# One more pair of row tiles per batch by half-size products in an attention and feed-forward block, with the turns and statistics moved to suit

## The chip, the cores and the metric

The kernel runs on one core of one Trainium2 chip. The metric is the device time of one execution in microseconds (us), of which the median over runs is given; lower is better. All arithmetic is 32-bit float. The core's engines each work through a list of instructions in order and wait for one another by semaphores: TensorE (PE in the profile, with PEld for its weight loads), VectorE (DVE), ScalarE (ACT), GpSimd (POOL) and SyncE (SP), which here only issues DMAs.

## What is computed

For each of 8 batches `b`, `x[b]` is 1024 x 256. The reference, cut to what matters:

```python
mod = (_silu(c) @ wmod).reshape(8, 6, 1, -1)
sa, ca, ga, sb, cb, gb = (mod[:, n] for n in range(6))     # ga, gb are kept away from zero
h = _layernorm(x) * (1 + ca) + sa
scores = einsum('nsd,ntd->nst', h * w_lhs, h * w_rhs)      # per batch 1024 x 1024
x = x + ga * einsum('nst,ntd->nsd', softmax(scores), h)
h = _layernorm(x) * (1 + cb) + sb
x = x + gb * (relu(h @ W1 + b1) @ W2 + b2)                 # 256 -> 1024 -> 256
```

## The kernel before, in words

**Tiles and order.** A batch has eight row tiles `i` of 128 rows, in two halves `g` of four (TH = 4). The loop at the end of the kernel goes over `b`, then over `i`, and in step (b, i) it writes out, in the order in which they are to run, the scores of tile i + 2 (`direct`, with `mirror`, since the scores are symmetric), the maximum (`row_max`), its turn onto columns by PE (`max_turn`), `subtract` and `exponent` of tile i + 1, the attention product of tile i, and a part of the feed-forward network (FFN) of the batch before: steps 0, 1 do its first product for half 0 (four chunks `c`, two in each step), steps 2, 3 its second product, steps 4 to 7 the same for half 1. The last batch's FFN runs after the loop. `pin` at the end ties each engine's instructions to the order in which they were written, so no scheduler changes it: what is behind a waiting instruction on its engine waits too. In batch 0 the attention is done differently and is not touched.

**The attention product.** `product(b, i)` (lines 486 to 499) multiplies the weights `pT` of one tile, as eight blocks of 128 x 128, with eight tiles of `xg`, 257 columns wide (256 and a column of ones for the softmax's denominator), into `po`. `product_out` (501 to 510) divides on DVE, adds to `x` and takes the statistics of the row (`stats`, lines 236 to 240) for the second layernorm, into `mvb`.

**Pairs.** Two tiles can be done together by a scheme of Strassen's kind with seven half-size products. `paired` (519) says which: i % 4 >= 2, so tiles 2 and 3, and 6 and 7, in batches 1 to 7. `pair_begin` (534) does two of the products (`pp`) on the first tile's weights alone, `pair_begin_sum` (553) adds them on DVE into `W`; `left_sums` (558) makes on POOL, in place, four sums of the two tiles' weights, of 128 x 512 each; `pair_end` (570) does the other five products (`pq`, `pr`), whose other side `tsum` comes from `right_sums` (once per batch); `pair_out` (589) puts them together on DVE in eight instructions; `pair_stats` (616) takes the statistics of both.

**FFN.** `pair_products` (722) does for one chunk the six products pa, pa, pb, pb, pc, pc and calls `between`, which holds the next `max_turn`, between pb and pc; ACT copies `pa` to `kept` (737); `pair_sums` (745) makes four DVE sums, `pair_last` (763) one more product, a DVE sum (769) and a POOL sum (770); `pair_relu` is ACT (779, 780), `pair_turn` (784) four POOL sums. The second product is `y_first`, `y_first_sums`, `y_second`, `y_second_sums` (843: two ACT instructions on Y). `y_turn` (848) transposes Y on DVE in blocks of 32 into a tile `T_y`, and `move` (296) sends it over DRAM: four DMAs out, one back, all issued by SP. With `hurry` the read back is issued at once, otherwise with the next move that hurries. `y_add` (860) adds it to `x` on POOL, `y_out` (868) stores.

**Turn buffers.** The tiles T of all transposes (`T_a`, `T_f`, `T_y`, `Tm`; lines 318, 429, 851) share one tag with two buffers, so a transpose waits until the DMAs out of the tile before the last have landed. PSUM tiles `pa`, `pb`, `pc`, `pp`, `pq`, `pr`, `po`, `ya` to `yd` share the four banks of the pool `ps_a`.

**The next batch's preparation** lies in the same steps: statistics at i = 1 and 3 (`prepare_stats`), the norm on ACT at i = 2 and 3 (`prepare_norm`, line 279), the turn and move (`prepare_blocks`) at i = 2 for half 0 and i = 4 for half 1, and the scaling on ACT (`prepare_turn_apart`, 340) at i = 4 and 5. `later` puts POOL work in a queue from which `spare` takes one piece.

Of the kernel before, what the change touches and what calls it, by code (L numbers as in the profile page):

```python
# [24 lines left out]
def adaln_block_kernel(  # L25
# [288 lines left out]
    def turn_blocks(src, name, X=None):  # L314

        T = two.tile([P, NV, NT * V], F32, tag="T", name=f"T_{name}")
        for k in range(ND):
            nc.vector.transpose(  # L320
                T.rearrange("p b (k t v) -> p k b t v", k=ND, v=V)[:, k],
                src(k).rearrange("p t (b v) -> p b t v", v=V),
            )
        if X is None:
            X = two.tile([P, NV, NT * V], F32, tag="X", name=f"X_{name}", bufs=1)
        move(X, T, NT * V, name)
        return X.rearrange("p a (k t v) -> p k t a v", k=ND, v=V)
# [94 lines left out]
    def mirror(b, i):  # L422
        if i == NT - 1:
            return
        n = NT - 1 - i
        if b == 0:
            mirror_first(i)
            return
        T = two.tile([P, NV, NT * V], F32, tag="T", name=f"Tm_{b}_{i}")
        T = T.rearrange("p b m -> p (b m)")[:, : NV * n * V].rearrange(  # L430
            "p (b m) -> p b m", b=NV
        )
        nc.vector.transpose(  # L433
            T.rearrange("p b (j v) -> p b j v", v=V),
            sc_t[b][:, i + 1 :, :, i, :].rearrange("p j b v -> p b j v"),
        )
        move(
            sc_t[b][:, i, :, i + 1 :, :].rearrange("p a j v -> p a (j v)"), T, n * V,
            f"m{b}_{i}",
        )  # L440
# [41 lines left out]

    mvb_t, po_t = {}, {}

    def product(b, i, parts=(0, 1)):
        pT = pT_t[b, i]
        if 0 in parts:
            po_t[b, i] = ps_a.tile([P, HALF], F32, tag="a", name=f"po_{b}_{i}")
        po = po_t[b, i]
        if 1 in parts:  # L490
            pT_t.pop((b, i))
        for t in [t for p in parts for t in range(p * TH, (p + 1) * TH)]:
            nc.tensor.matmul(  # L493
                po[:, : D + 1],
                lhsT=pT[:, t, :],
                rhs=xg_t[b][:, t, 0 : D + 1],
                start=(t == 0),
                stop=(t == NT - 1),
            )

    def product_out(b, i):
        po = po_t.pop((b, i))
        g, j = divmod(i, TH)
        if j == 0:
            mvb_t[b, g] = work.tile([P, TH, 2], F32, tag="mvb", name=f"mvb_{b}_{g}")
        rl = work.tile([P, 1], F32, tag="rl", name=f"rl_{b}_{i}")
        nc.vector.reciprocal(rl, po[:, D : D + 1])
        x2 = x_tile(b, i)
        nc.vector.scalar_tensor_tensor(x2, po[:, :D], rl, x2, ALU.mult, ALU.add)  # L509
        stats(mvb_t[b, g], j, x2, f"b{b}_{i}")  # L510

# [2 lines left out]
    XS = D - P + 1  # L516
    tsum = const.tile([P, 4, TH, P + 4], F32, name="tsum")
    nc.gpsimd.memset(tsum[:, 1, :, P : P + 1], 1.0)
    paired = lambda b, i: b > 0 and i % TH >= 2

    def right_sums(b, which):

# [47 lines left out]
    def pair_end(b, i):  # L570

        (s2, s4), (s3, a22) = halves(pT_t.pop((b, i))), halves(pT_t.pop((b, i + 1)))
        s1 = two_t.pop("s1")
        pq = ps_a.tile([P, HALF], F32, tag="a", name=f"pq_{b}_{i}")
        pr = ps_a.tile([P, HALF], F32, tag="a", name=f"pr_{b}_{i}")
        for out, lhs, rhs in (
            (pr[:, P : 2 * P], s1, tsum[:, 0, :, 0:P]),
            (pr[:, 2 * P : 3 * P], s3, tsum[:, 2, :, 0:P]),
            (pq[:, 0:XS], s2, tsum[:, 1, :, 0:XS]),
            (pq[:, XS : XS + P], a22, tsum[:, 3, :, 0:P]),  # L580
            (pr[:, 0:P], s4, xg_t[b][:, TH:NT, 0:P]),
        ):
            for t in range(TH):
                nc.tensor.matmul(  # L584
                    out, lhsT=lhs[:, t, :], rhs=rhs[:, t, :],
                    start=(t == 0), stop=(t == TH - 1),
                )
        two_t[b, i] = two_t[b, i][0], pq, pr
# [26 lines left out]

    def pair_stats(b, i):
        two_t.pop((b, i))
        g, j = divmod(i, TH)
        for q in range(2):
            stats(mvb_t[b, g], j + q, x_tile(b, i + q), f"b{b}_{i + q}")  # L620


    ffn = {}
# [96 lines left out]
    def pair_products(b, g, c, between=None):  # L720
# [12 lines left out]
        pc = ps_a.tile([P, HALF], F32, tag="a", name=f"pc_{b}_{g}_{c}")  # L733
        mm(pa[:, lo], w1[:, 0, n], hT[:, 0, lo])
        mm(pa[:, hi], s1, hs[:, 0])
        kept = work.tile([P, HALF], F32, tag="kept", name=f"kept_{b}_{g}_{c}", bufs=3)
        nc.scalar.copy(kept, pa)  # L737
        mm(pb[:, lo], w1s[:, 0, n], hs[:, 1])
        mm(pb[:, hi], w1s[:, 1, n], hs[:, 2])
        if between:  # L740
            between()
        mm(pc[:, lo], w1[:, 1, n], hT[:, 1, lo])
        mm(pc[:, hi], a22, hT[:, 0, hi])
        pairs[c] = pa, pb, pc, kept

    def pair_sums(b, g, c):
# [101 lines left out]
    def y_turn(b, g, hurry=False):  # L848

        Y = ffn["Y"]  # L850
        T = two.tile([P, NV, NT * V], F32, tag="T", name=f"T_y{b}_{g}")
        for h in range(2):
            nc.vector.transpose(
                T.rearrange("p a (t h u) -> p a t h u", h=2, u=V)[:, :, :, h, :],
                Y[:, h].rearrange("p (t a v) -> p a t v", a=NV, v=V),
            )
        Y = Y.rearrange("p h r -> p (h r)").rearrange("p (b m) -> p b m", b=NV)
        move(Y, T, NT * V, f"y{b}_{g}", hurry)
        ffn["rows", b, g] = Y.rearrange("p b (t h u) -> p t h b u", h=2, u=V)
# [239 lines left out]
    def middle(b, i):  # L1099

        if i == 0:
            ffn_norm(b - 1, 1)
        elif i == (6 if b < B - 1 else 4):
            ffn_norm(b, 0)

    def norms(b, i):
# [9 lines left out]
        elif b + 1 < B:  # L1116
# [3 lines left out]
            elif i == 2:  # L1120
                prepare_blocks(b + 1, 0)
                x_plus(b + 1, 0)
                xg_times(b + 1, 0)
        elif i == 4:

            ffn_blocks(b, 0)
        if b == B - 1:
# [12 lines left out]
    for b in range(B):  # L1140
        for i in range(NT):
# [59 lines left out]
            if first:  # L1201
# [3 lines left out]
                pair_products(fb, fg, c, turn_max)  # L1205
                if i == 0:
                    ffn_rstd(b - 1, 1)
                elif (b, i) == (B - 1, TH):
                    ffn_rstd(b, 0)
                if (b, i) == (1, 0):  # L1210
                    weights(*late)
                    late = None
# [3 lines left out]
                if ahead:  # L1216
                    mirror(*ahead)
                pair_last(fb, fg, c)
                if i == 0 and back:
                    for q in range(2):  # L1220
                        y_add(ub, ug, q)
                if i == TH + 1:
                    pair_turn(c - 1)
                if i == 4 and b + 1 < B:
                    prepare_blocks(b + 1, 1)
                    xg_times(b + 1, 1)
                if late:
                    subtract(*late)
                pair_products(fb, fg, c + 1, (lambda: max_turn(*extra)) if extra else None)
                if i == 5 and b + 1 < B:  # L1230
                    prepare_turn_apart(b + 1, 1, 1)
                    prepare_turn_apart(b + 1, 1, 0)
                pair_relu(c)
                sides_too = i == 4 and b + 1 < B
                if sides_too:
                    prepare_turn_apart(b + 1, 0, 1)
                if late:
                    exponent(*late)
                if sides_too:
                    prepare_turn_apart(b + 1, 0, 0)  # L1240
                middle(b, i)
                pair_sums(fb, fg, c + 1)
                pair_last(fb, fg, c + 1)
                if ahead and ahead != extra:
                    row_max(*ahead)
                pair_turn(c)
# [10 lines left out]
            else:  # L1257
                half = i % TH - 2
                if i == 3 and b + 1 < B:
                    prepare_stats(b + 1, 1)  # L1260
                if half == 0:
                    if i == 2:
                        pair_begin(b, i, turn_max)
                    else:
                        pair_begin(b, i, lambda: (max_turn(*late), weights(*late)))
                elif not ahead:

                    pair_end(b, i - 1)
                    pair_out(b, i - 1)
                    pair_stats(b, i - 1)  # L1270
                if half:
                    y_second(fb, fg, turn_max)
                else:
                    y_first(fb, fg)
                if i == NT - 2 and (b, 2) in two_t:
                    pair_stats(b, 2)
                if ahead:
                    mirror(*ahead)
                if i == 2 and b + 1 < B:
# [4 lines left out]
                    ffn_rstd(b, 0)  # L1284
                elif i == NT - 1 and b == B - 1:
                    ffn_rstd(b, 1)
                if half == 0:
                    pair_begin_sum(b, i)
                    if i == 2:
                        weights(*late)  # L1290
                    left_sums(b, i)
                spare()
                early(b, i)
# [22 lines left out]
            if not first:  # L1316
                if i == NT - 1 and b < B - 1:
                    y_turn(fb, fg, True)
                for _ in range(4 if half else 1):
                    spare()  # L1320
            if first:
                product(b, i)
                product_out(b, i)
            elif half and ahead:
                pair_end(b, i - 1)
                pair_out(b, i - 1)
                if i < NT - 1:
                    y_turn(fb, fg)
                if i == NT - 1:
                    assert not queue  # L1330
                    right_sums(b + 1, range(3))
                if i == NT - 1 or b == B - 1:
                    pair_stats(b, i - 1)
            late = ahead if ahead != extra else None
            if first and back:
# [82 lines left out]
```

## Time and profile before

| what | value |
|---|---|
| median of 3 runs | 772.51 us (772.37 to 774.09) |
| profiled execution, its own time | 774.46 us |
| its span in the trace | 772.7 us |
| PE busy | 759.6 us (98%) |
| DVE, POOL, ACT busy | 565.1, 538.2, 375.4 us |
| granted TensorE clock | 1.0 throughout |

One 32-bit product of the program is two PE instructions in the profile, so `product` shows as 16. Durations of one instruction overlap with the next; where times are added up, the distance from one start to the next is used. Times in the trace are us from the start of the span.

### The profile page before, as it was taken

To read this page: it belongs to the slowest core of one execution; us is meant where nothing else is said; L and a number is where in the kernel's file an instruction comes from. 1 tells how busy PE (TensorE), PEld (TensorE's weight loads), DVE (VectorE), ACT (ScalarE), POOL (GpSimd) and SP (SyncE) were. 2 spreads that over 40 slices of the span, in tenths; PEclk is the share of its full clock that TensorE was granted. 3 is DMA by queue.
4 is the path that set the end of the run, shared out by engine and by line. 5 is a ranking of instruction groups with operands and counts; after the bars stand their busy time and mean duration, and the time that the engine had idled before them with its cause. 6 is when DMAs were issued, how large, how long until landed. Compare 5 with 4: busy or idle time off the path is not lost.

```text
span 772.7 us, 11479 instructions
## 1 busy us (share of the span) xinstructions
PE 759.6 (98%) x3708; PEld 621.8 (80%) x3708; DVE 565.1 (73%) x1222; ACT 375.4 (49%) x681; POOL 538.2 (70%) x632
## 2 busy tenths in 40 slices
PE   8999999999999999999999999999999999999998
PEld 3576788788887888778887888878888788889886
DVE  6697878768785887758787687876878677595632
ACT  3464546635456355645546444563546535251511
POOL 4543974978849686596867787497884969559641
PEclk9999999999999999999999999999999999999999
DMA  5314335356443554434543554436534254142220
GB/s 193 123 50 145 106 103 133 101 176 170 123 122 101 171 143 113 140 95 151 156 126 118 150 150 130 117 101 192 167 93 130 87 167 142 35 115 98 81 83 27
DMA packets 106211, 95.18 MB, mean 123 GB/s; under 512 B 29700, under 2 KB 98848, under 8 KB 106152
## 3 DMA queue, kind: packets, MB, share of 16 engines
q1 hardware_dynamic: 98408, 85.81, 38.0%
q10 hardware_dynamic: 7744, 8.65, 3.7%
q8 instruction: 29, 0.48, 0.3%
q14 instruction: 30, 0.25, 0.1%
HBM read 50.62 MB, written 43.81 MB: 122 GB/s over the span
## 4 chain that ended last, share of the span: by engine, by line
PE 78%; DVE 10%; POOL 4%; DMA 3%; issue 2%; SPq 1%; ACT 1%; DVEq 0%; POOLq 0%
PE psc L410 14%; PE po L493 12%; PE pa L718 7%; PE yc L796 6%; PE ya L796 6%; PE yb L796 6%; PE pc L718 5%; PE pr L584 5%; PE pb L718 4%; PE pq L584 3%; PE py L901 3%; PE yd L796 3%; PE pp L544 3%; DMA D_y<-T_y 2%; DVE pT L472 1%
## 5 line engine op out<-in xcount | busy, mean ns | idle before, releaser
L770 POOL TENSOR_TENSOR f<-f,kept 128x512 f32<-128x512 f32 x64 | 81.5, 1273 | 116.7 <-DVE f L769 84.6
L410 PE MATMUL psc<-rT,lT 128*128 128x512 f32 (+3 forms) x384 | 134.6, 487 | 0.0
L493 PE MATMUL po<-xg,pT 128*128 128x257 f32 x576 | 131.6, 380 | 0.0
L493 PEld LDWEIGHTS po<-xg,pT 128*128 128x128 f32 x576 | 108.9, 190 | 15.9 <-issue 1.0
L472 DVE TENSOR_TENSOR pT<-sc,pm 128x1024 f32<-128x1024 f32 x64 | 77.1, 1205 | 30.7 <-PE pm L465 24.8
L410 PEld LDWEIGHTS psc<-rT,lT 128*128 128x128 f32 x384 | 67.7, 191 | 37.9 <-issue 26.3
L417 ACT COPY sc<-psc 128x512 f32<-128x512 f32 (+3 forms) x96 | 44.9, 475 | 104.0 <-PE psc L410 94.5
L481 ACT ACTIVATE pT<-pT 128x1024 f32<-128x1024 f32 x64 | 67.3, 1052 | 33.8 <-DVE pT L472 33.8
L460 DVE TENSOR_REDUCE m<-sc 128x1 f32<-128x1024 f32 x64 | 77.3, 1207 | 0.0
L737 ACT COPY kept<-pa 128x512 f32<-128x512 f32 x64 | 37.4, 584 | 78.2 <-PE pa L718 78.2
L779 ACT ACTIVATE f<-f 128x512 f32<-128x512 f32 x64 | 40.1, 627 | 62.4 <-POOL f L770 62.4
L718 PE MATMUL pb<-hs,w1s 128*128 128x256 f32 x256 | 66.0, 380 | 0.9 <-DVE f L755 0.8
L718 PE MATMUL pc<-hT,w 128*128 128x256 f32 x256 | 65.8, 380 | 0.0
L634 POOL TENSOR_TENSOR x<-x,rows 128x256 f32<-128x256 f32 x64 | 45.3, 739 | 22.3 <-DVE x L509 11.8
L718 PEld LDWEIGHTS pb<-hs,w1s 128*128 128x128 f32 x256 | 47.8, 190 | 9.1 <-DVE f L755 2.0
L718 PEld LDWEIGHTS pc<-hT,w 128*128 128x128 f32 x256 | 46.7, 192 | 6.9
L796 PE MATMUL yc<-f,w2s 128*128 128x256 f32 x224 | 52.1, 379 | 0.0
L796 PEld LDWEIGHTS yc<-f,w2s 128*128 128x128 f32 x224 | 41.5, 190 | 10.1 <-issue 2.9
L433 DVE STREAM_TRANSPOSE Tm<-sc 128x896 f32<-128x896 f32 (+6 forms) x49 | 34.6, 707 | 13.3 <-ACT sc L417 12.4
L790 POOL TENSOR_TENSOR ft<-ft,f 128x256 f32<-128x256 f32 x56 | 40.8, 728 | 4.4
L791 POOL TENSOR_TENSOR ft<-ft,f 128x256 f32<-128x256 f32 x56 | 40.8, 728 | 4.4
L789 POOL TENSOR_TENSOR ft<-f 128x256 f32<-128x256 f32 x56 | 40.9, 731 | 0.0
(165 smaller groups left out, 1672.7 us busy)
## 6 DMA issues: line engine op xcount, KB each, us to landing
D_f<-T_f SPq DMA_DIRECT2D x60, 128.0 KB, 2.7
X_f<-D_f SPq DMA_DIRECT2D x15, 512.0 KB, 3.7
D_a<-T_a SPq DMA_DIRECT2D x56, 128.0 KB, 3.2
D_y<-T_y SPq DMA_DIRECT2D x56, 128.0 KB, 2.6
Y<-D_y SPq DMA_DIRECT2D x14, 512.0 KB, 3.5
out_dram<-x SPq DMA_DIRECT2D x14, 512.0 KB, 3.0
X_a<-D_a SPq DMA_DIRECT2D x13, 512.0 KB, 3.4
x<-in_L_attn_x_dram ACTq DMA_DIRECT2D x12, 512.0 KB, 4.6
```

Of the source, the lines that this page charges most:

```text
L410: nc.tensor.matmul(psc[:, : hi - lo], lhsT=lT_t[b, i // TH][:, k, ts(i % TH, P)], rhs=rT_t[b, n][:, k, lo - n * HALF : HALF], start=(k == ...
L417: nc.scalar.copy(score_row(b, i)[:, lo // V : hi // V, :], psc[:, : hi - lo].rearrange("p (n v) -> p n v", v=V),)
L460: nc.vector.tensor_reduce(m, score_row(b, i), AX.XY, ALU.max)
L472: nc.vector.tensor_tensor(pT.rearrange("p j (a v) -> p j a v", v=V), score_columns(b, i), pm[:, :P].rearrange("p (j a v) -> p j a v", j=1, ...
L481: nc.scalar.activation(pT_t[b, i], pT_t[b, i], AF.Exp)
L493: nc.tensor.matmul(po[:, : D + 1], lhsT=pT[:, t, :], rhs=xg_t[b][:, t, 0 : D + 1], start=(t == 0), stop=(t == NT - 1),)
L584: nc.tensor.matmul(out, lhsT=lhs[:, t, :], rhs=rhs[:, t, :], start=(t == 0), stop=(t == TH - 1),)
L634: queue.append(lambda: nc.gpsimd.tensor_tensor(out, in0, row, op))
L718: nc.tensor.matmul(out, lhsT=lhsT, rhs=rhs, start=True, stop=True)
L770: nc.gpsimd.tensor_tensor(f[:, c::NH, hi], f[:, c::NH, hi], kept[:, None, hi].to_broadcast([P, 2, H2]), ALU.add,)
L789: add(ft[:, 0, c], f[:, c + NH, hi], f[:, c, hi], ALU.subtract)
L796: nc.tensor.matmul(out, lhsT=lhs(c), rhs=rhs(c), start=(c == 0), stop=(c == NH - 1))
```

## The change

Tiles 1 and 2, 3 and 4, 6 and 7 of batches 1 to 7 are done as pairs; tiles 0 and 5 by `product`. The middle pair spans both halves, so its statistics go to two tiles of `mvb`. `left_sums(b, 1)` stands at the start of step 2, `pair_end(b, 1)` at the end of step 2, `pair_begin(b, 3)` at the start of step 3, `pair_end(b, 3)` at the end of step 4. `y_turn` of half 0 goes from the end of step 3 into step 4, after the first chunk's `pair_last`; `prepare_blocks(b + 1, 1)` and `weights` (subtract and exponent) of tile 5 go behind the second chunk's `pair_last` of step 4; the exponent of tile 6 goes to before the scaling in step 5. T gets three buffers, `kept` two in place of three (one chunk of the last batch takes the buffer of `s1`), `between` is called after pc, the order of two products in `pair_end` changes, and in the last batch the norm of half 0 goes from step 4 to step 5.

```diff
-        T = two.tile([P, NV, NT * V], F32, tag="T", name=f"T_{name}")
+        T = two.tile([P, NV, NT * V], F32, tag="T", name=f"T_{name}", bufs=3)
...
+    def mvb_of(b, g):
+        if (b, g) not in mvb_t:
+            mvb_t[b, g] = work.tile([P, TH, 2], F32, tag="mvb", name=f"mvb_{b}_{g}")
+        return mvb_t[b, g]
...
-    paired = lambda b, i: b > 0 and i % TH >= 2
...
             (pr[:, P : 2 * P], s1, tsum[:, 0, :, 0:P]),
+            (pq[:, XS : XS + P], a22, tsum[:, 3, :, 0:P]),
             (pr[:, 2 * P : 3 * P], s3, tsum[:, 2, :, 0:P]),
             (pq[:, 0:XS], s2, tsum[:, 1, :, 0:XS]),
-            (pq[:, XS : XS + P], a22, tsum[:, 3, :, 0:P]),
...
-        g, j = divmod(i, TH)
-        for q in range(2):
-            stats(mvb_t[b, g], j + q, x_tile(b, i + q), f"b{b}_{i + q}")
+        for t in (i, i + 1):
+            stats(mvb_of(b, t // TH), t % TH, x_tile(b, t), f"b{b}_{t}")
...
-        kept = work.tile([P, HALF], F32, tag="kept", name=f"kept_{b}_{g}_{c}", bufs=3)
+
+        tag, bufs = ("s1", 1) if b == B - 1 and c % 3 == 2 else ("kept", 2)
+        kept = work.tile([P, HALF], F32, tag=tag, name=f"kept_{b}_{g}_{c}", bufs=bufs)
...
+        mm(pc[:, lo], w1[:, 1, n], hT[:, 1, lo])
+        mm(pc[:, hi], a22, hT[:, 0, hi])
         if between:
             between()
-        mm(pc[:, lo], w1[:, 1, n], hT[:, 1, lo])
-        mm(pc[:, hi], a22, hT[:, 0, hi])
...
-        elif i == (6 if b < B - 1 else 4):
+        elif i == (6 if b < B - 1 else 5):
             ffn_norm(b, 0)
...
-        elif i == 4:
+        elif i == 5:
             ffn_blocks(b, 0)
...
                 pair_last(fb, fg, c)
+                if (b, i) == (B - 1, 5):
+                    ffn_rstd(b, 0)
+                if i == 4:
+                    y_turn(fb, 0)
...
-                if i == 4 and b + 1 < B:
-                    prepare_blocks(b + 1, 1)
-                    xg_times(b + 1, 1)
-                if late:
+                if late and i != 4:
                     subtract(*late)
                 pair_products(fb, fg, c + 1, (lambda: max_turn(*extra)) if extra else None)
-                if i == 5 and b + 1 < B:
-                    prepare_turn_apart(b + 1, 1, 1)
-                    prepare_turn_apart(b + 1, 1, 0)
+                if i == 5:
+                    exponent(*late)
+                    if b + 1 < B:
+                        prepare_turn_apart(b + 1, 1, 1)
+                        prepare_turn_apart(b + 1, 1, 0)
...
-                if late:
+                if late and i not in (4, 5):
                     exponent(*late)
...
                 pair_last(fb, fg, c + 1)
+                if i == 4:
+                    if b + 1 < B:
+                        prepare_blocks(b + 1, 1)
+                        xg_times(b + 1, 1)
+                    weights(*late)
...
-                if half == 0:
-                    if i == 2:
-                        pair_begin(b, i, turn_max)
-                    else:
-                        pair_begin(b, i, lambda: (max_turn(*late), weights(*late)))
+                if i == 2:
+                    left_sums(b, 1)
+                elif i == 3:
+                    pair_begin(b, i, turn_max)
+                elif i == 6:
+                    pair_begin(b, i, lambda: (max_turn(*late), weights(*late)))
...
-                    y_second(fb, fg, turn_max)
+                    y_second(fb, fg, turn_max if i == NT - 1 else None)
                 else:
-                    y_first(fb, fg)
-                if i == NT - 2 and (b, 2) in two_t:
-                    pair_stats(b, 2)
+                    y_first(fb, fg, turn_max if i == 2 else None)
+                if i == NT - 2 and (b, 3) in two_t:
+                    pair_stats(b, 3)
...
-                if half == 0:
+                if i in (3, 6):
                     pair_begin_sum(b, i)
-                    if i == 2:
-                        weights(*late)
+                if i == 2:
+                    weights(*late)
+                elif i == 6:
                     left_sums(b, i)
...
-            if first:
+            if i in (0, 5):
                 product(b, i)
                 product_out(b, i)
-            elif half and ahead:
+            elif i == 1:
+                pair_begin(b, i)
+                pair_begin_sum(b, i)
+            elif i == 3:
+                left_sums(b, i)
+            elif i in (2, 4) or i == NT - 1 and ahead:
                 pair_end(b, i - 1)
                 pair_out(b, i - 1)
-                if i < NT - 1:
-                    y_turn(fb, fg)
                 if i == NT - 1:
                     assert not queue
                     right_sums(b + 1, range(3))
-                if i == NT - 1 or b == B - 1:
+                if i != 4 or b == B - 1:
                     pair_stats(b, i - 1)
```

More of the change, by code (lines that the diff above doesn't have):

```diff
@@ L428, in mirror @@
             return
-        T = two.tile([P, NV, NT * V], F32, tag="T", name=f"Tm_{b}_{i}")
+        T = two.tile([P, NV, NT * V], F32, tag="T", name=f"Tm_{b}_{i}", bufs=3)
         T = T.rearrange("p b m -> p (b m)")[:, : NV * n * V].rearrange(
@@ L503, in product_out @@
         g, j = divmod(i, TH)
-        if j == 0:
-            mvb_t[b, g] = work.tile([P, TH, 2], F32, tag="mvb", name=f"mvb_{b}_{g}")
         rl = work.tile([P, 1], F32, tag="rl", name=f"rl_{b}_{i}")
@@ L509, in product_out @@
         nc.vector.scalar_tensor_tensor(x2, po[:, :D], rl, x2, ALU.mult, ALU.add)
-        stats(mvb_t[b, g], j, x2, f"b{b}_{i}")
+        stats(mvb_of(b, g), j, x2, f"b{b}_{i}")
     XS = D - P + 1
@@ L850, in y_turn @@
         Y = ffn["Y"]
-        T = two.tile([P, NV, NT * V], F32, tag="T", name=f"T_y{b}_{g}")
+        T = two.tile([P, NV, NT * V], F32, tag="T", name=f"T_y{b}_{g}", bufs=3)
         for h in range(2):
@@ L1207, in adaln_block_kernel @@
                     ffn_rstd(b - 1, 1)
-                elif (b, i) == (B - 1, TH):
-                    ffn_rstd(b, 0)
                 if (b, i) == (1, 0):
```

## The prediction

> **What bounds the kernel now.** I read first the page's busy shares, then the chain that ended last, then the timeline of PE for gaps, then the timelines of ACT and POOL in the steps that are moved.
>
> ```profile
> PE 759.6 (98%) x3708; PEld 621.8 (80%) x3708; DVE 565.1 (73%) x1222; ACT 375.4 (49%) x681; POOL 538.2 (70%) x632
> ```
>
> PE is the bound. The chain, in order of time in batches 1 and 2 (start, length, what), is a row of PE products with nothing between them:
>
> ```profile
> 147.10 0.89 PE pp L544 x8
> ...
> 148.10 0.89 PE pp L544 x8
> ...
> 164.20 1.78 PE pr L584 x16
> 165.99 1.79 PE pq L584 x16
> 167.77 0.89 PE pr L584 x8
> ...
> 177.40 3.47 PE po L493 x16
> ```
>
> Here stand the prices of the change: a full product 3.47 us, a pair 0.89 + 0.89 + 1.78 + 1.79 + 0.89 = 6.24 us. Where PE does wait, the PE timeline says for what (in brackets), and the list of waits names the cause:
>
> ```profile
> 318.23 0.70 PE L718 MATMUL pa<-hT,w 128*128 128x256 f32 x2 [1.52 <-DVE f L755]
> ...
> 320.41 0.32 PE L465 MATMUL pm<-ident,m 128*128 128x128 f32 x1 [0.19 <-DVE m L460]
> ```
> ```profile
> DVE T_a L320 <- DMA D_y<-T_y: 11.6, 6, 3.3
> ```
>
> In step 4 of batches 1 to 6 DVE stands at the turn T_a until the DMAs of T_y free its buffer, and PE comes to wait for DVE in step 5. From start to start PE loses there 0.35 us in each of the six (2.1 in all), and where the DMAs were slow 1.68 more in batch 3, 0.54 in batch 5 and 0.64 (on ACT) in batch 6; in batch 7 it loses 0.95 at 680.71, also to DVE.
>
> Two stretches of batch 2 that the change meets with less room, ACT in step 3 and POOL in steps 1 to 2:
>
> ```profile
> 209.35 1.06 ACT L481 ACTIVATE pT<-pT 128x1024 f32<-128x1024 f32 x1 [1.04 <-DVE pT L472]
> 210.32 2.06 ACT L279 ACTIVATE xg<-x,rs,ra 128x256 f32<-128x256 f32 x4
> 212.29 1.50 ACT L843 ACTIVATE Y<-Y,gcol 128x512 f32<-128x512 f32 x2
> 215.12 0.37 ACT L417 COPY sc<-psc 128x256 f32<-128x256 f32 x1 [1.33 <-PE psc L410]
> 215.99 0.58 ACT L737 COPY kept<-pa 128x512 f32<-128x512 f32 x1 [0.49 <-PE pa L718]
> ```
> ```profile
> 197.26 0.73 POOL L792 TENSOR_TENSOR f<-f 128x256 f32<-128x256 f32 x1
> ...
> 200.01 1.27 POOL L564 TENSOR_TENSOR s<-pT 128x512 f32<-128x512 f32 x1 [1.98 <-ACT pT L481]
> 201.36 1.27 POOL L565 TENSOR_TENSOR pT<-pT,pT 128x512 f32<-128x512 f32 x1
> 202.71 1.27 POOL L566 TENSOR_TENSOR pT<-s,pT 128x512 f32<-128x512 f32 x1
> ```
>
> ACT has Y done 1.33 us before the next score copy is there to do, because `pair_end` of tiles 2-3 (4.46 us) lies between; POOL is free 1.98 us before the weights come.
>
> **What the Trainium skill says.** Perfetto Trace Analysis, Optimizing Scalar/DVE Operations: the latency that a profile shows of a DVE or ACT instruction overlaps with the next one. The trace agrees (`exponent` lasts 1.06 us, its follower starts after 0.97), so I add starts to starts. The same page, Optimization Strategy: the same gap repeating on the engine that should be full can mean too few buffers for the next tile; that is the wait of T_a, 11.6 us in six. DMA: Bandwidth & Descriptors, Anatomy of one DMA: about 2.0 us fixed, plus bytes over 436 GB/s, which makes 3.2 us for 512 KB as an estimate; the trace has 3.5 (Y) and 3.4 (X_a). GPSIMD Engine Reference, Engine selection: two-input sums are about twice as slow there as on VectorE; the trace has 0.73 us against 0.41 for 128 x 256.
>
> **Part 1, products.** 7 batches x (2 x 3.47 - 6.24) = 7 x 0.70: 4.9 us less on PE, all on the path.
>
> **Part 2, waits that go.** With three T buffers T_a waits for the DMAs of Tm of tile 5, long landed; `pm` after pc comes 0.86 us later. So the 2.1, the 1.68 + 0.54 + 0.64 and batch 7's 0.95 go: 5.9 us. The third buffer, the smaller `kept` (its POOL readers are done a step earlier) and the two `mvb` tiles cost no instruction. The statistics of tiles 1-2 are in (b) below; those of 3-4 take the place of those of 2-3 in step 6, the same four instructions.
>
> **Part 3, new waits.** Per batch DVE gets `pair_begin_sum` and `pair_out` (2.5 us) for two `product_out` less statistics (1.3), ACT a copy of 0.27, POOL 4 x 1.35 = 5.4 us of `left_sums`. The busy totals allow it (DVE 565 + 8, POOL 538 + 38, of 772). But they lie in steps 1 to 4, and there PE has 3.5 us less: step 1 has pp (1.78) for a product (3.47), and pp of the old pair (1.89 with pm) leaves step 2. I set 0 at the end of step 1's FFN products (189.02 in batch 2) and follow batch 2's durations for batches 1 to 6.
>
> (a) *POOL, end of step 2.* `pair_turn` of chunk 3 ends at 8.97, in all six batches within 0.05. Then `left_sums`: four starts 1.35 apart, the last done at 14.35. PE: pp 1.78, scores 1.72, y_first 6.91, pm 0.11, four fifths of `pair_end` 3.57: at 14.07 it needs that sum. Wait 0.34 with the semaphore. `pair_end` ends at 15.3.
>
> (b) *DVE and ACT, into step 4.* From 15.5 DVE does `pair_out` 2.25, two statistics 1.1, four of the next batch 2.1, Tm 0.37, W 0.25, reaching `subtract` of tile 4 at 21.65 (1.1 to 1.2): `exponent` at 22.88, norm 23.85, Y 25.82, score copy 27.25, `kept` 27.53, done 28.1. PE, unstalled: 15.3 + scores 1.29 + pp and pm 1.89 + y_second 5.18 + scores 0.86 + chunk 0 2.59 + pm 0.11 = 27.22, when `pair_last` needs `kept`. Wait 0.95. The cover, `pair_end` between Y and these copies, is gone.
>
> (c) *`pair_end` in step 4* finds `pr`'s bank free after chunk 0's L769, but `pq`'s only after chunk 1's second sum. DVE after `kept`: four sums 1.65, Tm, L769 and the moved T_y (1.25): chunk 1's sums begin at 31.65, the second ends at 32.65; PE comes at 32.54. Wait 0.15. In step 5 DVE is behind by T_a, subtract, row_max and `pair_out`; chunk 3's pb waits about 0.2.
>
> (d) *POOL, step 6.* The moved T_y ends at 31.65; SP has Tm's four issues and the read of the scores (to 33.7) ahead of D_y, then D_a's four (to 37.4), waits for their landing, reads X_a at about 40.4, and only behind it Y at 40.8. Y lands at 44.4 to 45.3 (two reads of 512 KB together; alone 3.5). `y_add` stands on POOL in front of chunks 2 and 3 of step 5, which take 11.35 us from its end to the last `pair_turn` (232.81 to 244.15 in batch 2; there Y waits for nothing). It ends 2.5 us after the landing, so the last relu is ready at 53.3 to 54.2, PE needs it at 53.15, and the last turned sum 0.4 later than PE: wait 0.5 to 1.4, I take 0.95.
>
> Sum per batch 0.34 + 0.95 + 0.15 + 0.2 + 0.95 = 2.6; six batches 15.6. Batch 7 prepares nothing: (a) 0.34, (b) and (c) 0.5 together, (d) nothing, since Y is read without X_a ahead: 0.85. The tail with its `kept` in two buffers and the norm one step later: 0 (products come 2.6 us apart or more there, and the norm has two steps left).
>
> **Sum.** Span 772.7 - 4.9 - 5.9 + 15.6 + 0.85 = 778.3; with the 1.8 around the span, 780.1 against 774.46 of the profiled execution. That execution was 1.95 above the median, and the three gaps from slow DMAs (2.86) differ from batch to batch; I count half of them for a median execution, so the gain is 1.4 smaller: 772.5 + 5.6 + 1.4 = **779.5**. Bounds: (a) 0 to 0.6, (b) 0.4 to 1.5 (starts of `subtract` 0.5 either way), (c) 0 to 0.8, (d) 0 (Y lands at 44) to 3 (each read slows the other fully); per batch 0.4 to 5.9, hardly all at one end.
>
> **Rivals.** *The room is enough* (not slower): the one place that decides is `subtract` of tile 4 in step 3. If DVE reaches it 1 us before 21.65, so that `kept` is done by 27.2, (b) is nothing, T_y and Y's DMAs come 1 us earlier, and (d) falls to nothing with it; only (a) is left. For it: DVE is 73% busy, and subtract of tile 3 waits for PE or DMA, so there is slack before. Against: from `pair_out` on, its list has no wait that could shrink. 772.5 - 4.9 - 5.9 + 1.4 + 7 x 0.4 = 766. *Half*: (b) stands, (d) doesn't, or the other way: 6 x 1.5 + 0.85 in place of 16.45: 773. *Y comes late*: (d) at 3 us because the reads and the store of x collide: 6 x 2 more, 791. For it, 4.04 us for D_y at 310.69, twice its usual 2.3.
>
> **How the numbers follow.** Forecast 0.50 (775 to 786), room enough 0.20 (763 to 770), half 0.18 (771 to 774.8), Y late 0.12 (787 to 795). The range of 8 in 10 takes in the forecast, half, and the near ends of the others: 767.5 to 788; the likeliest case alone 775 to 786. A measurement of this kernel can tell about 0.3%, 2.3 us: faster 0.20, same 0.18, slower 0.62.
>
> **What would show it.** In the profile after: `po` 352 PE instructions in place of 576, `pp` 336; no wait of T_a on D_y; PE waiting for POOL at `pr` in step 2, for ACT's `kept` at chunk 0's last product in step 4, and for ACT's relu of chunk 3 in step 6; POOL's L866 waiting for Y. If PE's busy share stays 98% and the second and third of these are missing, the forecast is wrong and the room was enough; if the third is over 2 us, Y came late.

## The result, and the profile after

| | before | after |
|---|---|---|
| median, 5 runs each on one chip | 772.37 us (771.67 to 774.09) | 784.83 us (783.88 to 785.44) |
| ratio after to before | | 1.0155 (95% interval 1.0141 to 1.0170) |
| profiled execution, its own time | 774.46 us | 783.88 us |
| its span | 772.7 us | 782.1 us |

The change makes the kernel 1.55% slower; the forecast was slower, at 779.5 us. The page has less work on PE and more on POOL, as counted, and one group, the sums of Y on POOL, that now waits for long (columns of the second line: instructions, busy us, mean ns, us of idle time before them and what ended it):

```profile
PE 758.5 (97%) x3876; PEld 622.7 (80%) x3876; DVE 569.0 (73%) x1257; ACT 376.1 (48%) x688; POOL 574.5 (73%) x660
...
L869 POOL TENSOR_TENSOR x<-x,Y 128x512 f32<-128x512 f32 x28 | 35.1, 1276 | 50.3 <-DMA Y<-D_y 50.3
```

PE's busy time fell by only 1.1 us, since a busy PE also contains slow starts: a product of `pa` lasts 0.70 us right behind the first wait below, and 0.59 without one. I split PE's time from start to start instead: each form's usual distance, times its count, gives about 750.6 us before and 745.8 after (4.8 less); what exceeds that, from PE's first start to its last end, is waiting and slow starts, about 17.4 us before and 31.5 after. Where it waits in batch 6 (PE timeline, brackets: us idle and what ended it):

```profile
593.84 0.70 PE L719 MATMUL pa<-hT,w1s 128*128 128x256 f32 x2 [0.87 <-ACT kept L740]
...
620.41 0.70 PE L799 MATMUL ya<-f,w 128*128 128x256 f32 x2 [1.62 <-ACT f L782]
620.95 1.89 PE L799 MATMUL yb<-f,w 128*128 128x256 f32 x8
623.37 1.97 PE L799 MATMUL ya<-ft,w2s 128*128 128x256 f32 x8 [0.53 <-POOL ft L792]
```

and in batch 2 at the pair of tiles 1 and 2, where POOL's fourth sum ends just behind PE:

```profile
204.58 1.09 PE L586 MATMUL pq<-tsum,pT 128*128 128x129 f32 x8
205.85 1.16 PE L586 MATMUL pr<-xg,pT 128*128 128x128 f32 x8 [0.18 <-POOL pT L569]
```

From start to start PE loses there 0.35 us in each of seven batches (2.4 in all), 1.03 at `kept` in each of six (6.1), and in step 6 from 0.8 to 2.7 in each of six and 0.6 in batch 7 (10.1, with the pauses of about 0.1 right behind the waits). The chain that ended last had PE in 78% of the span before; now PE has 42% and POOL 27%. In batch 6 it runs over POOL (the chain, in order of time):

```profile
602.96 0.69 POOL f L795
603.65 8.09 issue
...
611.77 2.49 POOL x L869 x2
614.26 1.22 POOL f L773
```

The 8.09 us named "issue" are POOL standing at the sums of Y (L869), which are next in its list; the list of waits says for what (us in total, times, longest), and no line in it has T_a waiting for D_y any more:

```profile
POOL x L869 <- DMA Y<-D_y: 50.3, 8, 8.1
```

SP's timeline of the same batch shows why Y is late. T_y's turn is done at 597.3, but its four writes stand behind the read of the scores, and Y's read stands behind the writes of T_a, their landing, and the read of X_a:

```profile
598.69 0.52 SPq L307 DMA_DIRECT2D sc<-D_m  x1
599.26 3.11 SPq L304 DMA_DIRECT2D D_y<-T_y  x4
602.41 1.89 SPq L304 DMA_DIRECT2D D_a<-T_a  x4
606.37 0.34 SPq L307 DMA_DIRECT2D X_a<-D_a  x1
607.14 0.34 SPq L307 DMA_DIRECT2D Y<-D_y  x1
```

The two stretches of batch 2 that the prediction showed as room look like this after. On ACT there is no idle time from `exponent` to `kept`:

```profile
214.59 1.06 ACT L481 ACTIVATE pT<-pT 128x1024 f32<-128x1024 f32 x1 [1.21 <-DVE pT L472]
215.55 2.06 ACT L279 ACTIVATE xg<-x,rs,ra 128x256 f32<-128x256 f32 x4
217.52 1.50 ACT L846 ACTIVATE Y<-Y,gcol 128x512 f32<-128x512 f32 x2
218.93 0.35 ACT L417 COPY sc<-psc 128x256 f32<-128x256 f32 x1
219.18 0.58 ACT L740 COPY kept<-pa 128x512 f32<-128x512 f32 x1
```

and on POOL `left_sums` follows the last turned sum with no gap:

```profile
199.62 0.73 POOL L795 TENSOR_TENSOR f<-f 128x256 f32<-128x256 f32 x1
...
200.34 1.28 POOL L566 TENSOR_TENSOR s<-pT 128x512 f32<-128x512 f32 x1
...
204.53 1.26 POOL L569 TENSOR_TENSOR pT<-pT 128x512 f32<-128x512 f32 x1
```

### The profile page after: what moved, and what is told of

Same layout as the page of the kernel before. It is cut to its first block, busy times and chain, and to the rows that moved or that the text cites. A ratio compares the mean times of both kernels' runs of the same rounds, so it can differ in the third digit from the quotient of the medians.

```text
span 782.1 us, 11913 instructions
## 1 busy us (share of the span) xinstructions
PE 758.5 (97%) x3876; PEld 622.7 (80%) x3876; DVE 569.0 (73%) x1257; ACT 376.1 (48%) x688; POOL 574.5 (73%) x660
## 4 chain that ended last, share of the span: by engine, by line
PE 42%; POOL 27%; DVE 14%; issue 10%; ACT 4%; DMA 2%; SPq 1%; DVEq 0%; POOLq 0%
PE psc L410 8%; POOL f L773 5%; PE po L498 5%; PE pr L586 4%; POOL ft L792 4%; PE yc L799 4%; PE pa L719 3%; POOL ft L793 3%; POOL ft L794 3%; PE py L904 3%; POOL f L795 3%; PE pb L719 3%; POOL x L869 3%; PE pc L719 2%; PE ya L799 2%
## 5 line engine op out<-in xcount | busy, mean ns | idle before, releaser
L498 PE MATMUL po<-xg,pT 128*128 128x257 f32 x352 | 80.7, 380 | 0.0
L498 PEld LDWEIGHTS po<-xg,pT 128*128 128x128 f32 x352 | 66.2, 190 | 10.0 <-issue 1.0
L869 POOL TENSOR_TENSOR x<-x,Y 128x512 f32<-128x512 f32 x28 | 35.1, 1276 | 50.3 <-DMA Y<-D_y 50.3
L719 PEld LDWEIGHTS pc<-hT,w 128*128 128x128 f32 x256 | 48.6, 190 | 6.6
L755 DVE SCALAR_TENSOR_TENSOR u<-pb,cols,kept 128x256 f32<-128x256 f32 x64 | 30.3, 473 | 28.3 <-ACT kept L740 16.7
L546 PEld LDWEIGHTS pp<-xg,pT 128*128 128x128 f32 x336 | 41.9, 192 | 5.1 <-issue 2.9
```

The lines of the kernel that those rows point to most:

```text
L498: nc.tensor.matmul(po[:, : D + 1], lhsT=pT[:, t, :], rhs=xg_t[b][:, t, 0 : D + 1], start=(t == 0), stop=(t == NT - 1),)
L546: nc.tensor.matmul(out, lhsT=lhs[:, t, :], rhs=xg_t[b][:, h * TH + t, P : P + XS], start=(t == 0), stop=(t == TH - 1),)
L719: nc.tensor.matmul(out, lhsT=lhsT, rhs=rhs, start=True, stop=True)
L869: nc.gpsimd.tensor_tensor(x2, x2, y, ALU.add)
```

## The experiments

The theory: the third pair's saving is real, and three waits that the moves and the pair create together outweigh it: for POOL's sums of the weights (2.4 us), for ACT's copy to `kept`, which stands behind Y in ACT's list (6.1), and for what is late behind POOL standing at the sums of Y (10.1). The rivals: that the load of the third pair on POOL and DVE is too much wherever things stand, and that the moves are the cause and the pair is innocent. Each time is compared with runs of the kernel before that were made beside it, since that kernel's own median moved between 771.9 and 773.2. "Over before" is the difference of the two medians.

| kernel | median us | ratio to before (95%) | over before, us |
|---|---|---|---|
| the change | 784.83 | 1.0155 (1.0141 to 1.0170) | +12.5 |
| e1 sums of Y later | 776.31 | 1.0040 (1.0027 to 1.0053) | +3.2 |
| e2 Y read first | 778.09 | 1.0059 (1.0046 to 1.0072) | +5.0 |
| e3 `kept` first | 777.71 | 1.0054 (1.0039 to 1.0070) | +4.6 |
| e4 before, three T | 772.30 | 0.9987 (0.9981 to 0.9994) | -0.8 |
| e5 = e1 and e3 | 769.65 | 0.9962 (0.9949 to 0.9974) | -2.7 |
| e6 = e5, a sum on DVE | 765.96 | 0.9915 (0.9902 to 0.9929) | -6.4 |
| e7 the change, two pairs | 778.35 | 1.0076 (1.0062 to 1.0090) | +6.0 |
| e8 = e4, exponent moved | 768.82 | 0.9953 (0.9940 to 0.9965) | -3.5 |
| e9 = e6, both ends mended | 763.73 | 0.9870 (0.9849 to 0.9892) | -9.4 |
| e10 = e9, two pairs | 768.64 | 0.9937 (0.9923 to 0.9951) | -4.5 |
| e11 the change, a copy on DVE | 782.98 | 1.0148 (1.0124 to 1.0172) | +11.1 |

**e1, the sums of Y later.**

```diff
-                elif back:                          # step 4, behind pair_turn(c)
-                    for q in range(2):
-                        y_add(ub, ug, q)
...
                 pair_last(fb, fg, c + 1)
...
+                if i == TH + 1:
+                    for q in range(2):
+                        y_add(ub, ug, q)
```

> The changed kernel with one thing moved: in batches 1 to 7 the two sums that add Y of half 0 to x (POOL) stand in step 5 behind the POOL sum of chunk 3, in place of the end of step 4, and the store of that half one step later. Theory (a POOL that stands at the head of its list waiting for the read of Y makes everything behind it late): the waits of PE in step 6 go, 4.4 us at the relu of chunk 3 and 4.7 us at the first product after the copy of Y, 9.1 in all with the rest of batch 7, so 784.8 - 9.1 = 775.7; the waits at the pair of tiles 1 and 2 (2.4 us) and at kept in step 4 (6.1 us) stay. Rival (POOL has simply too much work, 38 us more than before, and is late in step 6 whatever the order): the two sums still stand before the last turned sums, the wait for the relu goes but half of the other stays: 778 to 781. Rival (the store one step later delays the next load of x on ACT's queue): no better than 783.

It came to 776.31, 9.3 us better against before. In batch 6 the sums of Y wait for nothing, and the second products run without a gap:

```profile
605.61 1.27 POOL L773 TENSOR_TENSOR f<-f,kept 128x512 f32<-128x512 f32 x1
606.84 2.51 POOL L869 TENSOR_TENSOR x<-x,Y 128x512 f32<-128x512 f32 x2
```
```profile
611.31 1.89 PE L799 MATMUL ya<-f,w 128*128 128x256 f32 x8
613.03 1.89 PE L799 MATMUL yb<-f,w 128*128 128x256 f32 x8
614.76 1.89 PE L799 MATMUL ya<-ft,w2s 128*128 128x256 f32 x8
```

POOL's busy time is the same (574.7), so its load is not what was late in step 6: one waiting instruction was, with fourteen sums of three chunks, for the products of step 6, behind it. Batch 7, where Y came early, pays for the later place: PE waits there about 2 us in steps 6 and 7, 0.5 in the change (e9 puts that batch's sums back).

**e2, Y read first.** The same wait from its other end: only SP's order changes.

```diff
-                    y_turn(fb, 0)
+                    y_turn(fb, 0, True)
```

> The changed kernel with one thing moved: the read of Y of half 0 is issued right behind its own four writes, so that the four writes of T_a and the read of X_a come after it in SP's list. Theory (Y comes late because SP puts it behind the landing of D_a and behind X_a's issue): Y lands 3.5 to 4 us earlier, the waits in step 6 go or all but go, 9 us at most; X_a lands 3 to 4 us later and ACT's scaling in step 5 takes that over, which its slack before the relu of chunk 2 covers: 776 to 778. Rival (the two reads of 512 KB collide on the DMA engines and each takes longer, whatever the order): Y lands 1 us earlier, 780 to 783. Rival (X_a later makes the scores of the next batch late): 784 or more.

778.09: SP's order is why Y comes late, and turning it round has a price. PE waits no more for the relu, but X_a is late now, and ACT stands at the scaling. Batch 5:

```profile
515.91 1.52 ACT L340 ACTIVATE rT<-X_a,sides 128x512 f32<-128x512 f32 x2 [4.22 <-DMA X_a<-D_a]
```
```profile
516.78 1.99 PE L410 MATMUL psc<-rT,lT 128*128 128x512 f32 x4 [0.69 <-ACT rT L340]
```

PE loses 2.8 us at the scores in this profile: those of the next batch's first tile read `rT`, which that scaling makes. In e1 it loses nothing there. Moving the reader was better than moving the read, by 1.8 us.

**e3, `kept` first.**

```diff
-        for h in range(2):                          # end of y_second_sums
+    def y_scale(b):                                 # the same two instructions on Y
...
                 pair_products(fb, fg, c, turn_max)
+                if i == TH:
+                    y_scale(fb)
```

> The changed kernel with one thing moved: the two ACT instructions on Y of half 0 (1.5 us) stand in step 4 behind the copy to kept of chunk 0, in place of the end of step 3. Theory (PE waits at the last product of chunk 0 for kept because ACT's list has Y ahead of it): the 1.03 us of batches 1 to 6 go, 6.1 in all: 778.7. The turn of Y is as early as now, since DVE reaches it behind sums that themselves wait for kept, so the waits in step 6 stay as they are. Rival (the turn of Y now waits for ACT, so that Y lands later against PE, which is 1 us earlier): the wait in step 6 grows by what is won in step 4, 783 to 785. Rival (kept is late because DVE reaches the subtract late and everything of ACT shifts with it): half is won, 781 to 782.

777.71, 7.9 us better against before. The spans, 775.9 and 782.1, differ by 6.2, the size expected; the rest is 0.95, by which the change's profiled execution lies below its median, and 0.7, by which the kernel before was slower beside e3. The rivals, 781 and more, are out. ACT in batch 6 now:

```profile
586.65 0.35 ACT L417 COPY sc<-psc 128x256 f32<-128x256 f32 x1
586.91 0.58 ACT L740 COPY kept<-pa 128x512 f32<-128x512 f32 x1
587.38 1.52 ACT L849 ACTIVATE Y<-Y,gcol 128x512 f32<-128x512 f32 x2
```

`kept` starts 0.26 us behind the score copy and PE waits for it in no batch. The waits of step 6 are still there (10.9 us).

**e4 and e8, the kernel before with the third buffer.** e4 has the change's lines for T and `kept` and nothing else; e8 also the second of these edits:

```diff
-        T = two.tile([P, NV, NT * V], F32, tag="T", name=f"T_{name}")
+        T = two.tile([P, NV, NT * V], F32, tag="T", name=f"T_{name}", bufs=3)
...
-                if i == 5 and b + 1 < B:
-                    prepare_turn_apart(b + 1, 1, 1)
-                    prepare_turn_apart(b + 1, 1, 0)
+                if i == 5:
+                    exponent(*late)
+                    if b + 1 < B:
+                        prepare_turn_apart(b + 1, 1, 1)
+                        prepare_turn_apart(b + 1, 1, 0)
```

> The kernel before with the three turn buffers alone (and kept in two buffers, as in the change, to make the room). Theory of the prediction (the turn T_a waits for the DMAs of T_y and PE pays for it in step 5): 2.1 us go for certain, the 0.95 of batch 7 too, and of the 2.9 that slow DMAs cost in the profiled execution about half in a median one: 772.4 - 4.5 = 767.9. Rival (DVE is late there for its own work, the buffer is only what the profile names): 771 to 772.4. Rival (T_a earlier sends its DMAs into those of T_y and Y, and Y comes late for POOL): slower than 772.4.

> The kernel before with three turn buffers and one thing more of the change: the exponent of tile 6 stands on ACT ahead of the scaling of the next batch in step 5. With three buffers alone T_a no longer waits, but its DMAs still stand in SP's list behind the reads of the scores and of Y, so X_a lands no sooner, and ACT stands at the scaling with the exponent behind it: PE waits at the first product of the pair 6-7, 0.9 to 1.6 us in three batches of that profile. Theory (the stall only moved from DVE to ACT, and the two edits together remove it): 772.3 - 3 = 769. Rival (the scaling, later now by an exponent, makes the relu or the next batch's scores late): 772 or more.

e4 gained 0.8 us, not 4.5, so a step of the prediction was incomplete. T_a no longer waits in e4, yet SP still issues its writes behind the reads of the scores and of Y, so X_a lands no sooner, and now ACT stands there, with the exponent of tile 6 behind the scaling. ACT and PE of e4 in batch 6:

```profile
600.94 1.52 ACT L340 ACTIVATE rT<-X_a,sides 128x512 f32<-128x512 f32 x2 [4.84 <-DMA X_a<-D_a]
602.37 1.50 ACT L340 ACTIVATE lT<-X_a,sides 128x512 f32<-128x512 f32 x2
...
604.82 1.04 ACT L481 ACTIVATE pT<-pT 128x1024 f32<-128x1024 f32 x1
```
```profile
605.91 1.16 PE L544 MATMUL pp<-xg,pT 128*128 128x129 f32 x8 [1.43 <-ACT pT L481]
```

PE waits like this, 0.9 to 1.6 us, in three batches of that profile. With the exponent ahead of the scaling (e8) it waits in none of these places, and 3.5 us are won. The change has both edits, so this gain is in it; it belongs to the two together, since the exponent's move was not run alone. The missing 1.0 of the 4.5 is batch 7. PE still stands there for 0.95 us from start to start, in e4 and in e8 (this line):

```profile
674.84 1.13 PE L718 MATMUL pb<-hs,w1s 128*128 128x256 f32 x4 [0.79 <-DVE f L757]
```

Batch 7 prepares nothing, so it has no T_a, and DVE waits for no buffer: its list has `pair_out`, T_y and two statistics ahead of the sum that PE needs. Perfetto Trace Analysis in the Trainium skill (Optimization Strategy) says that a gap that repeats can mean too few buffers. The trace had such a gap, and the third buffer took away the wait named; alone it gave 0.8 us of the 3.5 that the two edits give, because a second thing, the order on ACT, was late by nearly as much.

**e5 and e6, the moves together.** e6 adds one edit to e5:

```diff
-        add(s1, a21, a22, ALU.add)
+        (nc.vector.tensor_tensor if i == 1 else add)(s1, a21, a22, ALU.add)
```

> The changed kernel with both moves that helped alone: the sums of Y of half 0 behind the POOL sum of chunk 3 in step 5, and ACT's two instructions on Y behind the copy to kept of chunk 0. Theory (the two waits are of different engines and add up): the 6.5 us that the first of these kernels still waits for kept go from its 776.3: 769.8. Rival (PE 1 us earlier in step 4 meets the next engine that is just in time, in step 5 or 6): 772 to 774. Rival (both moves freed the same waiting time): 776.

> The kernel with both moves, and the first of the four sums of the weights of tiles 1 and 2 done on DVE in place of POOL. Theory (the wait of 0.35 us at the last product of that pair is POOL's four sums in a row behind the last turned sums): 2.4 us go, 767.4 if both moves give 769.8. Rival (DVE has its own chain to subtract and kept in steps 2 to 4, and 0.7 us more there brings the wait for kept back): nothing is won, 769 to 771.

769.65 and 765.96. The two waits add up, and taking one of POOL's sums out of the row is worth 3.7 us, more than the 2.4 of the gaps (3.0 with the pauses behind them). e6's PE has no gap over 0.15 us from batch 2 to 6; what is left is at the ends: 1.16 us at batch 1's first pb, 2 in batch 7, and the tail.

**e7, two pairs with all the moves.**

```diff
-            if i in (0, 5):
+            if i in (0, 1, 2, 5):
                 product(b, i)
                 product_out(b, i)
-            elif i == 1:
-                pair_begin(b, i)
-                pair_begin_sum(b, i)
```

(and without `left_sums` and `pair_end` of tiles 1 and 2.)

> The changed kernel with tiles 1 and 2 done as two full products, so two pairs (3-4, 6-7) with all of the moves. Theory: PE has 7 x 0.70 = 4.9 us more to do; the wait at the pair of tiles 1 and 2 (2.4) goes with it; kept in step 4 is in time, since DVE has 2 us less to do behind step 2 (6.1 go); the wait for Y in steps 5 and 6 belongs to the moved turn and reads and stays (9.5): 784.8 + 4.9 - 2.4 - 6.1 = 781.2. Rival (the load of the third pair on POOL and DVE is the cause of all the new waits): 784.8 + 4.9 - 18 = 771.7. Rival (the moves are, not the pair): only the 2.4 go, 787.3.

778.35: between the theory and the rival of load, nearer the theory. The trace decides: the waits at `pr` and at `kept` are gone, as both of these said, and those of step 6 remain (9.6 us from start to start), which the rival denied. So in the prediction's terms (a) and (b) need the third pair, and (d) is there without it: it belongs to the moves, of which the middle pair's shift to tiles 3 and 4 is one. Of the 2.9 us under the theory's figure, 1.3 are the pauses behind the two waits, which go with them, and 0.5 is the shorter wait of step 6; most of the rest is again the 0.95 by which the change's profiled execution, from which the waits were taken, lies below its median.

**e9 and e10, the best version and the pair's price in it.**

```diff
+        if between and (b, g, c) == (0, 0, 0):      # ahead of pc
+            between()
...
-                    y_turn(fb, 0)
+                    y_turn(fb, 0, b == B - 1)
...
-                if i == TH + 1:
+                if i == TH + 1 and b < B - 1:       # last batch: y_add in step 4
```

> The kernel with both moves and the sum on DVE, and two small edits at its ends: in the first of batch 1's FFN products the turn of the maximum stands between pb and pc again (PE waits 1.16 us there, 0.30 before the change), and in the last batch the sums of Y stay at the end of step 4, with the read of Y issued at once. Theory: 0.86 goes in batch 1 and 1 to 1.5 of the 2 us that PE still waits in batch 7: 766.0 - 2.1 = 763.9. Rival (in batch 7 POOL is late for its load, wherever the sums of Y stand): 765.

> The last kernel with tiles 1 and 2 done as two full products. Theory (where nothing waits for the third pair, its price is PE's 0.70 us per batch and no more): 763.9 + 4.9 = 768.8. Rival (the pair costs more than its products show even there, by POOL's and DVE's extra work): 764 to 767.

763.73 and 768.64: e9 beats the kernel before by 1.3%, and between the two medians the third pair is worth 4.9 us, the seven times 0.70 of the products (the four executions of e9 spread over 1.7 us, the six of e10 over 0.5). The first line of the page of e9:

```profile
PE 752.8 (99%) x3876; PEld 623.9 (82%) x3876; DVE 577.3 (76%) x1264; ACT 374.8 (49%) x688; POOL 568.5 (75%) x653
```

POOL has 30 us more to do than before, DVE 12, and between the medians none of it is seen in the time.

**e11, who is late at the second wait of step 6.** The bracket at 623.37 above names a turned sum of POOL. In program order that product waits for two things: chunk 0's turned sum, done some 20 us before, and ACT's copy of `ya` to Y (L811), since it writes the other half of that tile. The same page of the skill (Optimization Strategy) says that it can make sense to check the source for the dataflow behind a wait; here that changed the name. In batch 7 of the change, where POOL is early, the bracket itself names the copy (0.52 us from start to start). ACT of the change in batch 6:

```profile
620.26 0.61 ACT L783 ACTIVATE f<-f 128x512 f32<-128x512 f32 x1
620.78 1.05 ACT L417 COPY sc<-psc 128x512 f32<-128x512 f32 x2
621.72 1.07 ACT L481 ACTIVATE pT<-pT 128x1024 f32<-128x1024 f32 x1
622.68 0.27 ACT L552 COPY W<-pp 128x129 f32<-128x129 f32 x1
622.83 0.39 ACT L811 COPY Y<-ya 128x256 f32<-128x256 f32 x1
```

```diff
-        nc.scalar.copy(Y[:, 0, lo], ya[:, lo])
+        (nc.vector.tensor_copy if g else nc.scalar.copy)(Y[:, 0, lo], ya[:, lo])
```

> The changed kernel with the copy of ya into Y in step 6 done by DVE in place of ACT. PE waits 0.69 us in each of batches 1 to 6, and 0.52 in batch 7, at the first product behind that copy; the profile names a turned sum of POOL, but the turned sum that this product reads was done some 17 us before (616 at the latest for the second chunk), and the copy ended 0.15 us before the product began. Theory (the copy of ACT, behind the late relu, two score copies and an exponent, is what PE waits for): 4.2 to 4.7 us go, 780.1 to 780.6; the wait at the relu itself stays. Rival (POOL's turned sums are late, as the prediction has it): the wait stays or moves to the second or third product of that group, 784 to 785.

782.98: 1.4 us better against before, less than expected, and the trace says that both were partly right. With the copy on DVE the product begins at once, and then the fourth of its group waits for POOL after all (batch 6 of e11):

```profile
621.12 0.42 DVE L811 COPY Y<-ya 128x256 f32<-128x256 f32 x1 [3.51 <-POOL ft L793]
```
```profile
622.60 2.27 PE L799 MATMUL ya<-ft,w2s 128*128 128x256 f32 x8
```
```profile
624.16 0.30 PEld L799 LDWEIGHTS ya<-ft,w2s 128*128 128x128 f32 x2 [0.51 <-POOL ft L793]
```

PE loses 0.21 to 0.28 there in six batches in place of 0.69. Two engines were late behind the same relu, ACT by 0.69 and POOL by 0.26, and the later hid the other. That makes about 3 us with batch 7; that the median shows only 1.4 goes with waits for the relu that are 1.2 us longer in this execution, and for `kept` 0.5 longer. Why they are longer is not shown.

## Why the prediction came out as it did

The direction held, and so did the mechanism of (a), (b) and the first half of (d); (c) was not there, and the second half of (d) was another engine's. The total is nearer than its terms, by luck: (c), 2.1 us too much, hid almost half of the 4.4 that (d) had too little. The sum was 3.8 us short for the span (778.3 against 782.1). The rest is how the medians stand to the profiled executions: I had the changed kernel's execution 0.55 above its median (before's 1.95, less 1.4), and it lies 0.95 below. 3.8 + 0.55 + 0.95 makes the 5.3 between 779.5 and 784.83. Times below "on the prediction's clock" count from the end of step 1's FFN products.

- *Part 1, products, 4.9 us less:* right. 4.8 in the trace, and 4.9 measured by itself (e10 against e9).
- *Part 2, waits that go, 5.9:* right in size, wrong for two of its reasons. "With three T buffers T_a waits for the DMAs of Tm of tile 5" gives only 0.8 by itself; it takes the exponent's move, to which I gave no value, to make 3.5 (e4, e8). And batch 7's 0.95 never was the buffer's: it is still there in e4 and e8. In the change it is gone because `pair_out` and T_y no longer stand in front of that sum.
- *Part 3 (a), 0.34 per batch:* right in size and cause: 0.344 to 0.369 in all seven, POOL named, and gone when one sum moves to DVE (e6). Pauses right behind it add 0.65 in all.
- *(b), 0.95 per batch:* right: 1.02 to 1.03 in six batches, and pauses of 0.1. `subtract` of tile 4, the place that was to decide against "room enough", started at 21.97 on the prediction's clock in batch 2, with no wait on DVE ahead of it from `pair_out` on, where I had 21.65 (my own addends make 21.57); PE came 0.2 later too. ACT's order is shown by e3. In e7, without the third pair, `exponent` starts 2.3 us earlier against PE and the wait is gone as well: the wait needs both, the late `subtract` and Y ahead of `kept`. Batch 7, with 0.5 for (b) and (c) together, has no wait for `kept`, and 0.24 at chunk 3's pb.
- *(c), 0.35 per batch:* wrong, nothing was there in batches 1 to 6. DVE's second sum of chunk 1 ends at 598.2 in batch 6, and PE comes for its bank at 598.29: in time by 0.1, where I had it late by 0.15. DVE was 0.1 later than I had it, but PE 0.3, by the longer (b) and the pauses that I had at nothing. This term was 2.1 us too much.
- *(d), 0.95 per batch:* right in the mechanism of its first half, too small. I had Y land at 44.4 to 45.3 on the prediction's clock; the sums of Y start 44.42 to 45.15 in batches 1 to 4, 46.27 and 46.35 in 5 and 6. In batch 6 the four writes of T_y took 3.11 to issue, not 2.06, and in batch 5 they began 1.6 later than elsewhere, because the read of the scores ahead of them did. These two batches lose 2.6 and 2.7 us, the others 0.8 to 1.5. The second half of the term was wrong in its engine: I had PE wait 0.4 for the last turned sum of POOL; it was 0.69, because ACT's copy of `ya`, behind the relu, two score copies and an exponent, comes later than that sum (e11). In all 10.1 for 5.7, of which batch 7, set at nothing, has 0.6.
- *The tail and `pm` behind pc, at nothing:* the tail yes. In batch 1, where `pm` in step 0 has a subtract on DVE behind it and ahead of the sums that free pb's bank, 0.86 came up that I had not counted; with `pm` ahead of pc in that one chunk it is gone (e9).
- *The rivals:* "half" and "room enough" fell with (b) and (d), both present in six batches. "Y comes late" did happen in two batches of six, near its 3 us, but from SP's order and late writes. That the reads slow each other was in the forecast, and shows alike in all six: Y lands about 4.1 to 4.6 us after its issue where X_a's read went out just before, and 3.1 to 3.2 in the second half, where none did. A collision with the store of x was not shown.

Still open is why SP's four writes of T_y differ by 1 us from batch to batch; e1 and e9 show how to be indifferent to it.

## What to carry to other kernels

A change that saves work on the full engine, as this one does, moves every other engine's deadline forward: follow the lists of the other engines to the next wait in front of a deadline, and look there at what stands first. An instruction that waits for a DMA belongs behind the work that does not need it. Here moving two sums on POOL by one step and two instructions on ACT by one place turned 1.5% slower into 0.4% faster, without taking any work away. Cover that is counted on for a stage (`pair_end` over ACT's list) should be named with its length, because a later edit may remove it.

## What the runs showed of the hardware beyond that

The first product after a wait is slower: behind the wait for `kept` in batch 6 the next product starts 0.54 us after it, against 0.43 without a wait; behind the waits of (a) and (b) these pauses make 1.3 us in all. And a bracket names the last event before a start: at 623.37 it named POOL's sum that ended 0.01 us before, while the copy that the product needed had ended 0.15 us before; in batch 7, where the copy is named, the product also starts 0.14 behind it.
